# Value products by seven multiplications with a transfer each way, and other places for a difference, loads, pieces and last additions

## The chip, the cores and the metric

The kernel runs on one core of one Trainium2 chip. The metric is device time in microseconds (us) of that core. Its engines have their own instruction streams and meet through semaphores: PE (TensorE, matmuls; PEld its weight loads), DVE (VectorE), ACT (ScalarE), POOL (GpSimd) and SP (SyncE, which here only issues transfers). An engine's stream is in order: an instruction that waits holds all behind it.

## The reference, cut to what matters

```python
def reference(x, Wqkv, Wout, w1, w2, w3):          # x: 1 x 2048 x 256
    xn = layernorm(x)
    qkv = einsum('bsd,ed->bse', xn, Wqkv)          # 16 heads of 128: q, k, v
    logits = einsum('bqhd,bkhd->bhqk', q, k) * 128 ** -0.5
    out = einsum('bhqk,bkhd->bqhd', softmax(logits), v)
    attn = einsum('bse,de->bsd', out, Wout)
    ffn = bitlinear(sigmoid(bitlinear(xn, w1)) * bitlinear(xn, w2), w3)
    return x + attn + ffn
```

All in float32. The change concerns `v`, the values: for each head a 2048x256 by 256x128 product.

## The kernel before, in words

**Stages.** A lead-in loads x, normalizes and transposes it into `xnT` (256 channels as 2 x 128 partitions, 2048 tokens), computes the feed-forward part and the first heads' q, k and v. The main loop (L905 to L1025) goes over 63 of the 64 blocks, and the last one follows it (`last_weighted`). Block n is head n // 4 and a quarter of 512 queries; it has four steps t = 0 to 3 of 128 queries each. Two heads are a group of eight blocks; below, "block i" is i = n % 8 within its group, and block 8 is block 0 of the next group.

**One step** of the loop does for a step six ahead (`LEAD`) the scores (PE: 16 matmul instructions of 512 columns into two of three PSUM tiles; DVE: two maxima and nm; ACT: two exponentials), then `exchanged` (twelve transfers of 64 KB, ten on SP's queue and two on ACT's, and four copies on ACT, which carry 32-row pieces between partitions), two steps later `transposed` (DVE, two transposes of 128x1024 into `R`), and for the step itself `weighted` (PE, probabilities by values).

**Seven products for eight.** The weighted sum is done by a scheme of Strassen's kind (Winograd's form): a 2x2 split needs seven products in place of eight and sums of the operands. On the side of the probabilities these are the differences T1 to T4 (`differences`), on POOL, in place in `R` (seven slots of 128x2048; `roles` says which slot is a, b, c, d, e of a block). On the side of the values they are `v_combined` 0 to 3, into `st` and in place. PE needs T1 and T2 in step 1 of a block, T3 in step 2, T4 in step 3. A block's POOL program is: in step 3 of the block before T1 (first half), T3 (first half) and, where a head begins, `v_combined` 0 and 1; in step 0 `put_away` (a transfer that waits for DVE's last operation on the block before), T1 (second half), `spread` (a transfer that broadcasts the inverse sums), T3 (second half), T2 (low); in step 1 T2 (high), `v_combined` 2 and 3 where a head begins, T4; in step 2 the transfer of `inverses`, which waits for DVE.

**What lies beside.** Each step can take one or two more products on PE, through one PSUM bank (`ps_m`, one buffer, so that a product waits until DVE has read the one before it). Steps 2 and 3 make the next head's q and k, by seven products as well (`fast_product`, `fast_read`, with sums of weights `ws` and of x `t0`, `t2`, made once by `x_sums`). Steps 0 and 1 make output products of the group before in blocks 0 to 3 (`o_product`), and the next group's values in blocks 4 to 7: `v_product` (L261), one a step, gives 256 tokens by 256 columns, for both heads, straight with tokens on partitions; `v_read` (L271) copies it into the two heads' value tiles.

A product's first half is issued inside `beside`, behind the step's scores; its second (`twice`) at the step's end, and the read of the second in `left` (`behind`), at the start of the next step, ahead of which comes `added` (DVE: the sum of the copied halves into `oU`, and in step 3 the multiplication by the inverses).

**Other things touched.** `between` (L875) issues most of POOL's transfers behind step t: weights, `o_fetched`, `y_moved`, and towards the end `fetched_back` (part sums back into `xnT`) and `x_fetched`. `first` (L869) places pieces of the first heads' q, k and v in the lead-in's last steps.

Of the kernel before, what the change touches and what calls it, by code (L numbers as in the profile page):

```python
# [9 lines left out]
F32 = mybir.dt.float32  # L10
F32R = mybir.dt.float32r
AF = mybir.ActivationFunctionType
ALU = mybir.AluOpType
# [7 lines left out]
def layernorm_attention_bitffn_kernel(  # L21
# [14 lines left out]
    nc = tc.nc  # L36
    P = 128
    S, DM = x.shape
    FF = w1T.shape[1]
    D = P  # L40
# [10 lines left out]
    G = 2  # L51
# [93 lines left out]
    def weight_sums(h: int):  # L145
# [6 lines left out]
        nc.gpsimd.tensor_tensor(w[:, 3], wk[:, 1], w[:, 1], sub)  # L152
        ws[h] = w

    def x_sums(c: int):
        t = apool.tile([P, 4, QB], F32, tag=f"t{c}", name=f"t{c}", bufs=1)
        x00, x10 = (xnT[:, d, bass.ts(c, QB)] for d in range(KC))
        x01, x11 = (xnT[:, d, bass.ts(c + 1, QB)] for d in range(KC))
        for i, (a, b) in enumerate(((x01, x00), (x11, t[:, 0]), (x11, x01), (x10, t[:, 1]))):
            nc.gpsimd.tensor_tensor(t[:, i], a, b, ALU.subtract)  # L160
        ts[c] = t

    def fast_product(h: int, b: int, i: int, second: bool):

        c = b // 2 * 2
        wk, wq = (weights[h // G, i][:, :, bass.ts(h % G, D)] for i in "kq")
        w, t = ws[h], ts[c]
        x00, x10 = (xnT[:, d, bass.ts(c, QB)] for d in range(KC))
        x11 = xnT[:, 1, bass.ts(c + 1, QB)]
        lhs, rhs = {  # L170
            (0, 0): ((wk[:, 0], x00), (w[:, 1], t[:, 1])),
            (0, 1): ((w[:, 2], t[:, 2]), (wq[:, 1], t[:, 3])),
            (1, 0): ((w[:, 0], t[:, 0]), (w[:, 3], x11)),
            (1, 1): ((wk[:, 1], x10),),
        }[b % 2, i][second]
        pm = ps_m.tile([P, QB], F32, tag="m", name=f"pw{h}_{b}_{i}_{int(second)}")
        in_halves(pm, lhs, rhs, True, True)
        return pm

    def fast_read(h: int, b: int, i: int, second: bool, pm):  # L180
        c = b // 2 * 2
        if (b % 2, i) == (0, 0):
            if not second:
                if c == 0:
                    kTs[h] = kvpool.tile([P, S], F32, tag="kT", name=f"kT{h}")
                for j in range(2):
                    qTs[h, c + j] = kvpool.tile(
                        [P, QB], F32, tag="qT", name=f"qT{h}_{c + j}", bufs=NB + 2
                    )
        k0, k1 = (  # L190
            kTs[h].rearrange("p (j k r) -> p k j r", j=P // 32, r=32)[:, j * TB : (j + 1) * TB]
            for j in (c, c + 1)
        )
        q0, q1 = qTs[h, c], qTs[h, c + 1]
        pk = pm.rearrange("p (k j r) -> p k j r", j=P // 32, r=32)
        def q_sum(q, base):
            nc.vector.tensor_tensor(q, pm, base, ALU.add)  # L197

        def k_sum(k, base):
            nc.vector.tensor_tensor(k, pk, base, ALU.add)  # L200

        if (b % 2, i) == (0, 0):
            if not second:
                nc.vector.tensor_copy(k0, pk)
            else:
                k_sum(k1, k0)
        elif (b % 2, i) == (0, 1):
            if not second:
                nc.vector.tensor_tensor(
                    q1.rearrange("p (k j r) -> p k j r", j=P // 32, r=32), pk, k1, ALU.add  # L210
                )
            else:
                q_sum(q0, q1)
        elif (b % 2, i) == (1, 0):
            if not second:
                q_sum(q1, q1)
            k_sum(k1, k1)
        else:
            k_sum(k0, k0)
# [38 lines left out]

    def v_product(g: int, m: int, second: bool):  # L261
        w = weights[g, "v"]
        pm = ps_m.tile([P, 2, G * D], F32, tag="m", name=f"pvw{g}_{m}")
        for j in range(2):
            for d in range(KC):
                in_halves(
                    pm[:, j], xnT[:, d, bass.ts(2 * m + j, P)], w[:, d], d == 0, d == KC - 1
                )
        return pm

    def v_read(g: int, m: int, second: bool, pm):  # L271
        for j in range(G):
            nc.vector.tensor_copy(
                v_tile(g * G + j)[:, 2 * m : 2 * m + 2], pm[:, :, bass.ts(j, D)]
            )

    ppool = ctx.enter_context(tc.tile_pool(name="ppool", bufs=2))
    front = ExitStack()
# [7 lines left out]
    ods = [  # L286
        [away.tile([P, G, QB], F32, tag=f"od{g}_{c}", name=f"od{g}_{c}") for c in range(NB)]
        for g in range(2)
    ]
    rds = [away.tile([P, 32], F32, tag=f"rd{i}", name=f"rd{i}") for i in range(2)]  # L290

# [292 lines left out]
    def exchanged(v: int):  # L584
        ps = exps.pop(v)
        parts[v] = [
            ppool.tile([P, 2, S // NQ], F32, tag=f"part{i}", name=f"part{v}_{i}") for i in range(2)
        ]


        todo = [(j + 2 * a, g + 2 * i) for a in range(2) for i in range(2) for j in range(2) for g in range(2)]
        def ends(j, g):
            return (
                parts[v][g // 2][bass.ts(j, 32), g % 2, :],
                ps[j // 2][bass.ts(g, 32), bass.ts(j % 2, S // NQ)],
            )

        for m, (j, g) in enumerate((j, g) for j, g in todo if j != g):
            queue = nc.sync if m < SP_DMAS else nc.scalar
            if v > len(blocks) * TB - 3:  # L600

                queue = (nc.sync, nc.scalar)[m % 2]
            queue.dma_start(*ends(j, g))  # L603
        for j in range(NQ):
            nc.scalar.copy(*ends(j, j))  # L605
# [227 lines left out]
    def projected(n: int, u: int, pool=ps_m, tag: str = "m"):  # L833
# [34 lines left out]

    first = {  # L869
        1: [("v", 0, NV - 1), ("k", 1, 0)], 2: [("k", 1, 1), ("q", 0, NB - 1)],  # L870
        3: [("k", 1, 2), ("q", 1, 1)], 4: [("k", 1, 3), ("q", 1, 2)], 5: [("v", 0, NV - 2)],
    }
    made = {("q", 1, 0)} | {p for todo in first.values() for p in todo}

    def between(n: int, t: int):  # L875

        g, i = divmod(n, GB)
        last = NBK - NB

        if t == 1:  # L880
            if i == NB - 1 and g + 1 < H // G:
                load_weights(g + 1, "v", nc.gpsimd)
            elif i == GB - 1 and n < last or n == last - 1:
                load_weights(g, "o", nc.gpsimd)
        if g and i < NB:
            if t == 0 and i + 1 < NB:
                y_moved(i + 1, False)
            elif t == 1 and i + 1 < NB:
                o_fetched(g - 1, i + 1)
        elif n < last:  # L890
            if (i, t) == ((GB - 2, 2) if g else (GB - 1, 2)):
                y_moved(0, False)
            if (i, t) == (GB - 2, 3):
                o_fetched(g, 0)
        if n >= last - 1 and t == (1 if n < last else 2):
            b = n + 1 - last
            nc.gpsimd.dma_start(o3[:, b % 2], ods[(H - 2) // G % 2][b][:, 0])
        if (n, t) in ((last - 2, 3), (last - 1, 2)):
            fetched_back(n + 2 - last)
        if t == 0 and n in (last - 3, last - 2, last, last + 1):  # L900
            x_fetched((last - 3, last - 2, last, last + 1).index(n))

    behind = []
    with tc.manual_schedule():
        for u in range(-LEAD, (NBK - 1) * TB):  # L905
# [13 lines left out]
            if n >= NB and t < 2:  # L919
                i, j = divmod(i, NB)  # L920
                j = 2 * j + t
                if not i:
                    seven, hi = True, (g - 1, j)
                    product, read, twice = o_product, o_read, False
                elif g + 1 < H // G:
                    seven, hi = True, (g + 1, j)
                    product, read, twice = v_product, v_read, False
            pms = []

            def beside():  # L930
# [10 lines left out]
            if t == 0 and n >= 0:  # L941
                if 0 < n <= NBK - NB:
                    put_away(n - 1)
                differences(n, "T1b")
                spread(n)
                differences(n, "T3b")
            elif t == 1 and n >= 0:
                differences(n, "T2h")
                if blocks[n][1] == 0:
                    v_combined(blocks[n][0], 2)  # L950
                    v_combined(blocks[n][0], 3)
                differences(n, "T4")
            elif t == 3 and -1 <= n < NBK - 2:
# [1 line left out]
                if n % GB < NB <= n < NBK - NB - 2:  # L955
                    y_moved(n % GB, True)
                differences(n + 1, "T3a")
                if n >= 0 and blocks[n + 1][1] == 0:
                    v_combined(blocks[n + 1][0], 0)
                    v_combined(blocks[n + 1][0], 1)  # L960
            if more:
# [21 lines left out]
                elif v % TB == 1 and ("q", 1, b) not in made:  # L983
                    q_piece(1, b)
            if b == NB - 1 and h + 2 < H:
                if h % G == 0 and v % TB in (0, 2):
                    load_weights(h // G + 1, "qk"[v % TB // 2], nc.gpsimd)
                if v % TB == 3:
                    weight_sums(h + 2)
            twice = seven and twice  # L990
# [21 lines left out]
            if more:  # L1012
                exchanged(v)
            if v == NBK * TB + 1:
                transposed(v - 3)
                transposed(v - 2)
            if t == 2 and n > NBK - NB:
# [7 lines left out]
                between(n, t)  # L1025

        n = NBK - 1
        behind.pop()()
        for k in range(NKT):
            last_weighted(k, 0)  # L1030
            if k in (KQ - 1, 3 * KQ - 1):
# [47 lines left out]
```

## Time and profile before

| what | value |
|---|---|
| runs | 2183.15, 2184.22, 2187.87 us; median 2184.22 |
| the profiled execution | 2184.97 us; its span, first to last instruction, 2183.2 us |
| granted clock of PE, mean | 0.998 |
| DVE transposes `R<-part`, 128x1024, x512 | 605.2 us busy, 1220 ns each |
| DVE `kT<-pw,kT`, 128x512 from PSUM, x112 | 76.9 us busy, 686 ns each |
| DVE `v<-pvw`, 128x256 from PSUM, x112 | 42.0 us busy, 417 ns each |
| POOL differences `R<-R`, 128x1024 and 128x2048, x441 | 1176.6 us busy |
| POOL waiting for DVE's `oU` before `od<-oU` | 192.6 us in 60 blocks |
| transfers on POOL's queue, 512 KB: `o<-od`, `osums<-yd`, `yd<-osums` | 4.2, 4.3, 3.4 us to landing (medians) |
| transfers `part<-p`, 64 KB, x2552 on SP and x520 on ACT | 2.2 and 2.1 us to landing |

A line of a timeline or a group reads: start and duration in us, engine, line of the code, operation, out<-in by the program's names, shapes, how many; in brackets the idle time before it and what ended it. A line of the list of waits reads: engine, what waited, what it waited for; us in all, times, the longest. Matmuls are pipelined and their ends are modelled, so PE's starts say more than its busy time. float32 matmuls appear as two instructions, and a product that is issued in two halves of 64 columns as four.

### The profile page before, as it was taken

The numbers are of one execution on the slowest core, as the hardware profiler recorded it, in microseconds if no ns is written. First come the engines' busy times: TensorE is split into PE (matmuls) and PEld (weight loads), VectorE is DVE, ScalarE is ACT, GpSimd is POOL, SyncE is SP. The second block draws the span as 40 slices with busy tenths as digits, with TensorE's granted clock in tenths as the row PEclk, the third lists the DMA queues.
The fourth block names the chain that finished last, engine by engine and source line by source line (L and its number), as shares of the span: only waits on it lengthen the run. The fifth ranks groups of instructions, "written<-read, shape, count | busy, mean of one in ns | idle before, by whom it ended". The sixth has DMA issues, their size and how long they took to land. (4 is left out here: it accounts for less than half of the span.)

```text
span 2183.2 us, 41234 instructions
## 1 busy us (share of the span) xinstructions
PE 2160.2 (99%) x14074; PEld 1412.8 (65%) x14074; DVE 1725.5 (79%) x2338; ACT 1374.6 (63%) x2414; POOL 1472.0 (67%) x884
## 2 busy tenths in 40 slices
PE   9998999999999999999999999999999999999998
PEld 6744567776666666666666666666666665666665
DVE  6567887888887887888788788788788878888774
ACT  5586666666666666666666666666666666666662
POOL 0067767767667766767777776786766777677772
PEclk9999999999999999999999999999999999999999
DMA  2155545665556655566555654566555665556652
GB/s 93 41 115 138 124 112 136 159 170 134 120 138 164 163 129 124 142 170 156 122 135 143 175 144 113 135 159 172 130 118 138 173 160 126 126 141 175 168 144 80
DMA packets 180771, 300.65 MB, mean 138 GB/s; under 512 B 54416, under 2 KB 59920, under 8 KB 180560
## 3 DMA queue, kind: packets, MB, share of 16 engines
q1 hardware_dynamic: 127472, 174.69, 31.7%
q0 software_dynamic: 27152, 88.30, 15.9%
q10 hardware_dynamic: 25936, 35.03, 6.4%
q8 instruction: 111, 1.82, 0.4%
q14 instruction: 100, 0.82, 0.1%
HBM read 61.93 MB, written 34.54 MB: 44 GB/s over the span
## 5 line engine op out<-in xcount | busy, mean ns | idle before, releaser
L669 POOL TENSOR_TENSOR R<-R 128x1024 f32<-128x1024 f32 x441 | 1176.6, 2679 | 115.5 <-DVE R L649 100.4
L94 PE MATMUL s<-kT,qT 128*64 128x512 f32 x4000 | 953.2, 593 | 2.1 <-ACT p L578 2.1
L605 ACT COPY part<-p 32x512 f32<-32x512 f32 x1024 | 630.7, 616 | 394.8 <-issue 269.9
L568 DVE TENSOR_REDUCE mx<-s 128x1 f32<-128x1024 f32 x512 | 620.6, 1222 | 300.7 <-PE s L94 287.1
L94 PEld LDWEIGHTS s<-kT,qT 128*64 128x64 f32 x4000 | 502.9, 137 | 308.5 <-issue 80.9
L578 ACT ACTIVATE p<-s,nm 128x1024 f32<-128x1024 f32 x512 | 565.9, 1110 | 209.1 <-PE pw L94 105.7
L649 DVE STREAM_TRANSPOSE R<-part 128x1024 f32<-128x1024 f32 x512 | 605.2, 1220 | 15.1 <-DMA part<-p 13.1
L716 PE MATMUL av<-R,v 128*64 128x256 f32 x3728 | 551.0, 379 | 0.1
L716 PE MATMUL av<-R,st 128*64 128x256 f32 x3024 | 471.7, 379 | 11.0 <-POOL R L669 9.0
L716 PEld LDWEIGHTS av<-R,v 128*64 128x64 f32 x3728 | 363.4, 137 | 160.3 <-issue 8.8
L716 PEld LDWEIGHTS av<-R,st 128*64 128x64 f32 x3024 | 304.2, 137 | 97.3 <-POOL R L669 13.0
L620 POOL DMA_DIRECT2D rd<-r x60 | 33.7, 562 | 233.9 <-DVE r L619 233.9
L734 ACT COPY oU<-av 64x256 f32<-64x256 f32 x248 | 90.7, 366 | 127.0 <-PE av L716 124.6
L772 POOL DMA_DIRECT2D od<-oU x60 | 34.0, 567 | 195.1 <-DVE oU L746 192.6
L742 DVE TENSOR_TENSOR oU<-av,oU 64x256 f32<-64x256 f32 x248 | 102.2, 412 | 45.5 <-ACT oU L734 42.8
L94 PE MATMUL pvw<-wv,xnT 128*64 128x256 f32 x896 | 117.7, 379 | 0.0
L94 PE MATMUL pow<-o,wo 128*64 128x512 f32 x448 | 116.1, 592 | 0.0
L94 PEld LDWEIGHTS pvw<-wv,xnT 128*64 128x64 f32 x896 | 78.6, 137 | 42.3 <-DVE qT L197 5.2
L94 PE MATMUL pw<-t,ws 128*64 128x512 f32 x336 | 105.3, 592 | 0.0
L578 ACT ACTIVATION_READ_ACCUMULATOR p<-s,nm 128x1 f32 x512 | 100.3, 196 | 0.0
L94 PEld LDWEIGHTS pow<-o,wo 128*64 128x64 f32 x448 | 58.9, 137 | 37.3 <-issue 5.4
L200 DVE TENSOR_TENSOR kT<-pw,kT 128x512 f32<-128x512 f32 x112 | 76.9, 686 | 1.7
(146 smaller groups left out, 1332.2 us busy)
## 6 DMA issues: line engine op xcount, KB each, us to landing
part<-p SPq DMA_DIRECT2D x2552, 64.0 KB, 2.2
part<-p ACTq DMA_DIRECT2D x520, 64.0 KB, 2.1
oT<-rd POOLq DMA_DIRECT2D x60, 256.0 KB, 5.6
od<-oU POOLq DMA_DIRECT2D x60, 256.0 KB, 2.7
o<-od POOLq DMA_DIRECT2D x28, 512.0 KB, 4.2
osums<-yd POOLq DMA_DIRECT2D x28, 512.0 KB, 4.3
yd<-osums POOLq DMA_DIRECT2D x26, 512.0 KB, 3.4
yd<-yT SPq DMA_DIRECT2D x4, 512.0 KB, 2.6
```

What stands on the lines that cost most here:

```text
L94: nc.tensor.matmul(out[c * HP : (c + 1) * HP], lhs[:, c * HP : (c + 1) * HP], rhs, start=start, stop=stop, skip_group_check=True,)
L200: nc.vector.tensor_tensor(k, pk, base, ALU.add)
L568: nc.vector.tensor_reduce(mx[:, i : i + 1], s, AX.X, ALU.max)
L578: nc.scalar.activation(p, s, AF.Exp, bias=nm, scale=SCALE, accum_out=sums[n][:, t, i : i + 1],)
L605: nc.scalar.copy(*ends(j, j))
L620: nc.gpsimd.dma_start(rds[n % 2], riT)
L649: nc.vector.transpose(to[:, t % 2, 2 * i : 2 * i + 2], part.rearrange("p g (s c) -> p g s c", s=2),)
L669: nc.gpsimd.tensor_tensor(o, x, y, ALU.subtract)
L716: nc.tensor.matmul(av[i * HP : (i + 1) * HP, half], l[:, kk], moving(s, kk), start=start, stop=(k == units[r] - 1), skip_group_check=True,)
L734: nc.scalar.copy(u[op, oq], av[ap, half])
L742: nc.vector.tensor_tensor(u[p, q], av[p, half], u[p, q], ALU.add)
L772: nc.gpsimd.dma_start(ods[h // G % 2][b][:, h % G], oU)
```

## The change

The values of a group are made by seven products for each half of the tokens (1024), in the form of `fast_product`: `fast_v_product`, with weight sums made by `v_sums` on POOL (four operations on 128x128) in step 3 of block 3, and the x sums that exist. A product is 128 channels by 512 tokens, so values come out with channels on partitions. `fast_v_read` adds each into the value tiles (eight operations of 128x512 a half). Then each head's half is turned: `v_sent` writes it to DRAM (512 KB, rows interleaved), `v_landed` reads it back into a part of `xnT` that is no longer read (`landing`: channels 0 to 127 of tokens 512 to 1535), both on POOL's queue, and `v_transposed` transposes its 32x32 blocks on DVE (two operations of 128x512). One landing place serves all four halves of a group, in turn; `v_steps` places them from block 5, step 1, to block 8, step 3. To leave tokens 512 to 1535 free, the second pair of token quarters is used in reverse order (`pair`).

Besides: `v_combined` 0 and 1 of a group's first head come after its last `v_transposed`; T3 (second half) and `spread` go from step 0 to step 1, behind T2 (high); the load of `wk` goes one step earlier; in the lead-in a piece of v and one of k change places; `fetched_back` and two loads into `o3` near the end go to other steps; the last `left` comes before the last transposes; the last two steps' exchanges use the queues as all others do.

```diff
+    def pair(c: int):
+        return (c, c + 1) if c == 0 else (c + 1, c)
...
-    def v_product(g: int, m: int, second: bool):
-        w = weights[g, "v"]
-        pm = ps_m.tile([P, 2, G * D], F32, tag="m", name=f"pvw{g}_{m}")
-        for j in range(2):
-            for d in range(KC):
-                in_halves(
-                    pm[:, j], xnT[:, d, bass.ts(2 * m + j, P)], w[:, d], d == 0, d == KC - 1
-                )
+    def sums_of(k, q, name: str):
+        w = wpool.tile([P, 4, D], F32, tag="wx", name=name)
+        nc.gpsimd.tensor_tensor(w[:, 0], q[:, 0], q[:, 1], ALU.add)
+        nc.gpsimd.tensor_tensor(w[:, 1], w[:, 0], k[:, 0], ALU.subtract)
+        nc.gpsimd.tensor_tensor(w[:, 2], k[:, 0], q[:, 0], ALU.subtract)
+        nc.gpsimd.tensor_tensor(w[:, 3], k[:, 1], w[:, 1], ALU.subtract)
+        wxs[name] = w
+    def fast_v_product(g: int, m: int, second: bool):
+        half, m = divmod(m, NB)
+        wv, w, t = weights[g, "v"], wxs[f"wvs{g}"], ts[2 * half]
+        c0, c1 = pair(2 * half)
+        x00, x10 = (xnT[:, d, bass.ts(c0, QB)] for d in range(KC))
+        x11 = xnT[:, 1, bass.ts(c1, QB)]
+        lhs, rhs = (
+            ((wv[:, 0, D:], x00), (w[:, 1], t[:, 1])),
+            ((w[:, 2], t[:, 2]), (wv[:, 1, :D], t[:, 3])),
+            ((w[:, 0], t[:, 0]), (w[:, 3], x11)),
+            ((wv[:, 1, D:], x10),),
+        )[m][second]
+        pm = ps_m.tile([P, QB], F32, tag="m", name=f"pvw{g}_{half}_{m}_{int(second)}")
+        in_halves(pm, lhs, rhs, True, True)
         return pm
...
+        todo = {
+            (0, True): ((k1, k0),), (1, False): ((q1, k1),), (1, True): ((q0, q1),),
+            (2, False): ((q1, q1), (k1, k1)), (2, True): ((k1, k1),), (3, False): ((k0, k0),),
+        }[m, second]
+        for o, i in todo:
+            nc.vector.tensor_tensor(o, pm, i, ALU.add)
+    def v_sent(h: int, half: int):
+        v = v_half(h, half).rearrange("p k d -> p (k d)")
+        nc.gpsimd.dma_start(
+            vds[h % G][half].rearrange("(r q) x -> q r x", q=P // 32), v
+        )
+    def v_landed(h: int, half: int):
+        nc.gpsimd.dma_start(landing, vds[h % G][half].rearrange("p (j c) -> j p c", j=P // 32))
+    def v_transposed(h: int, half: int):
+        v = v_half(h, half).rearrange("p k (q r) -> p q k r", r=32)
+        w = landing.rearrange("p (q k r) -> p q k r", q=P // 32, r=32)
+        for u in range(2):
+            nc.vector.transpose(v[:, 2 * u : 2 * u + 2], w[:, 2 * u : 2 * u + 2])
+    wxs, landing = {}, xnT[:, 0, QB : 3 * QB]
...
-            if v > len(blocks) * TB - 3:
-                queue = (nc.sync, nc.scalar)[m % 2]
...
-        3: [("k", 1, 2), ("q", 1, 1)], 4: [("k", 1, 3), ("q", 1, 2)], 5: [("v", 0, NV - 2)],
+        3: [("k", 1, 2), ("q", 1, 1)], 4: [("v", 0, NV - 2), ("q", 1, 2)], 5: [("k", 1, 3)],
...
+        v_steps = {
+            (5, 1): [(v_sent, 0, 0)], (5, 2): [(v_landed, 0, 0)],
+            (5, 3): [(v_transposed, 0, 0), (v_sent, 1, 0)],
+            (6, 1): [(v_landed, 1, 0)], (6, 2): [(v_transposed, 1, 0)],
+            (7, 1): [(v_sent, 0, 1)], (7, 2): [(v_landed, 0, 1)], (7, 3): [(v_transposed, 0, 1)],
+            (8, 1): [(v_sent, 1, 1)], (8, 2): [(v_landed, 1, 1)], (8, 3): [(v_transposed, 1, 1)],
+        }
...
+        for late in range(2):
+            if late < g + 1 < H // G + late:
+                for do, j, half in v_steps.get((i + late * GB, t), ()):
+                    do((g + 1 - late) * G + j, half)
+        if t == 3 and i == GB - 1 and g + 1 < H // G:
+            v_combined((g + 1) * G, 0)
+            v_combined((g + 1) * G, 1)
-        if n >= last - 1 and t == (1 if n < last else 2):
+        if n >= last - 1 and t == 2:
...
+        if t == 3:
+            if i == NB - 1 and g + 1 < H // G:
+                v_sums(g + 1)
-        if (n, t) in ((last - 2, 3), (last - 1, 2)):
+        if (n, t) in ((last - 2, 3), (last - 1, 0)):
             fetched_back(n + 2 - last)
...
-                    product, read, twice = v_product, v_read, False
+                    product, read, twice = fast_v_product, fast_v_read, j % NB != NB - 1
...
                 differences(n, "T1b")
-                spread(n)
-                differences(n, "T3b")
             elif t == 1 and n >= 0:
                 differences(n, "T2h")
+                differences(n, "T3b")
+                spread(n)
...
-                if n >= 0 and blocks[n + 1][1] == 0:
+                if n >= 0 and (n + 1) % GB == NB:
                     v_combined(blocks[n + 1][0], 0)
                     v_combined(blocks[n + 1][0], 1)
...
-                if h % G == 0 and v % TB in (0, 2):
-                    load_weights(h // G + 1, "qk"[v % TB // 2], nc.gpsimd)
+                if h % G == 0 and v % TB in (0, 1):
+                    load_weights(h // G + 1, "qk"[v % TB], nc.gpsimd)
...
             if v == NBK * TB + 1:
+                behind.pop()()
                 transposed(v - 3)
                 transposed(v - 2)
...
-        behind.pop()()
```

More of the change, by code (lines that the diff above doesn't have):

```diff
@@ L153, in weight_sums @@
         ws[h] = w
+    def pair(c: int):
+        return (c, c + 1) if c == 0 else (c + 1, c)
     def x_sums(c: int):
         t = apool.tile([P, 4, QB], F32, tag=f"t{c}", name=f"t{c}", bufs=1)
-        x00, x10 = (xnT[:, d, bass.ts(c, QB)] for d in range(KC))
-        x01, x11 = (xnT[:, d, bass.ts(c + 1, QB)] for d in range(KC))
+        c0, c1 = pair(c)
+        x00, x10 = (xnT[:, d, bass.ts(c0, QB)] for d in range(KC))
+        x01, x11 = (xnT[:, d, bass.ts(c1, QB)] for d in range(KC))
         for i, (a, b) in enumerate(((x01, x00), (x11, t[:, 0]), (x11, x01), (x10, t[:, 1]))):
@@ L167, in fast_product @@
         w, t = ws[h], ts[c]
-        x00, x10 = (xnT[:, d, bass.ts(c, QB)] for d in range(KC))
-        x11 = xnT[:, 1, bass.ts(c + 1, QB)]
+        c0, c1 = pair(c)
+        x00, x10 = (xnT[:, d, bass.ts(c0, QB)] for d in range(KC))
+        x11 = xnT[:, 1, bass.ts(c1, QB)]
         lhs, rhs = {
@@ L191, in fast_read @@
             kTs[h].rearrange("p (j k r) -> p k j r", j=P // 32, r=32)[:, j * TB : (j + 1) * TB]
-            for j in (c, c + 1)
+            for j in pair(c)
         )
-        q0, q1 = qTs[h, c], qTs[h, c + 1]
+        q0, q1 = (qTs[h, j] for j in pair(c))
         pk = pm.rearrange("p (k j r) -> p k j r", j=P // 32, r=32)
@@ L255, in v_place, with v_sums @@
         return (k + NKT // 2) % NKT if h == 1 else k
-    def v_product(g: int, m: int, second: bool):
-        w = weights[g, "v"]
-        pm = ps_m.tile([P, 2, G * D], F32, tag="m", name=f"pvw{g}_{m}")
-        for j in range(2):
-            for d in range(KC):
-                in_halves(
-                    pm[:, j], xnT[:, d, bass.ts(2 * m + j, P)], w[:, d], d == 0, d == KC - 1
-                )
-        return pm
[L271 to L274, printed above, removed]
-            )
+    def v_sums(g: int):
+        wv = weights[g, "v"]
+        sums_of(wv[:, :, D:], wv[:, :, :D], f"wvs{g}")
@@ new lines, in sums_of @@
+    def sums_of(k, q, name: str):
[9 more added lines that the diff above has]
+        c0, c1 = pair(2 * half)
+        x00, x10 = (xnT[:, d, bass.ts(c0, QB)] for d in range(KC))
+        x11 = xnT[:, 1, bass.ts(c1, QB)]
+        lhs, rhs = (
[6 more added lines that the diff above has]
+        in_halves(pm, lhs, rhs, True, True)
+        return pm
@@ new lines, in v_half, with fast_v_read @@
+    def v_half(h: int, half: int):
+        return v_tile(h)[:, half * NKT // 2 : (half + 1) * NKT // 2]
+    def fast_v_read(g: int, m: int, second: bool, pm):
+        half, m = divmod(m, NB)
+        q, k = (
+            v_half(g * G + i, half).rearrange("p k d -> p (k d)").rearrange(
+                "p (j k r) -> p k j r", j=P // 32, r=32
+            )
+            for i in range(G)
+        )
+        k0, k1, q0, q1 = (
+            i[:, j % 2 * TB : (j % 2 + 1) * TB] for i in (k, q) for j in pair(2 * half)
+        )
+        pm = pm.rearrange("p (k j r) -> p k j r", j=P // 32, r=32)
+        if (m, second) == (0, False):
+            nc.vector.tensor_copy(k0, pm)
+            return
+        todo = {
[4 more added lines that the diff above has]
+            nc.vector.tensor_tensor(o, pm, i, ALU.add)
@@ new lines, in v_sent @@
+    def v_sent(h: int, half: int):
+        v = v_half(h, half).rearrange("p k d -> p (k d)")
+        nc.gpsimd.dma_start(
+            vds[h % G][half].rearrange("(r q) x -> q r x", q=P // 32), v
+        )
+    def v_landed(h: int, half: int):
[5 more added lines that the diff above has]
+            nc.vector.transpose(v[:, 2 * u : 2 * u + 2], w[:, 2 * u : 2 * u + 2])
@@ L288, in layernorm_attention_bitffn_kernel @@
         for g in range(2)
+    ]
+    vds = [
+        [away.tile([P, S // 2], F32, tag=f"vd{h}{i}", name=f"vd{h}{i}") for i in range(2)]
+        for h in range(G)
     ]
```

## The prediction

> **What bounds the kernel now.** I read the page's busy line first, then the list of waits, then the timelines of the places where the change acts.
>
> ```profile
> PE 2160.2 (99%) x14074; PEld 1412.8 (65%) x14074; DVE 1725.5 (79%) x2338; ACT 1374.6 (63%) x2414; POOL 1472.0 (67%) x884
> ...
> L94 PE MATMUL pvw<-wv,xnT 128*64 128x256 f32 x896 | 117.7, 379 | 0.0
> ```
>
> PE is the bound: time falls only if PE gets less work or loses a stall. The list of waits says how few stalls there are, and which reads are just in time:
>
> ```profile
> PE av L716 <- POOL R L669: 9.0, 8, 3.3
> ...
> PEld pow L94 <- DVE qT L197: 4.6, 13, 0.4
> ```
>
> PE's starts give each product's price better than its busy time, since matmuls overlap:
>
> ```profile
> 305.89 2.09 PE L94 MATMUL pvw<-wv,xnT 128*64 128x256 f32 x16
> 307.62 3.82 PE L716 MATMUL av<-R,st 128*64 128x256 f32 x32
> ...
> 641.60 1.23 PE L94 MATMUL pw<-xnT,ws 128*64 128x512 f32 x4
> 642.46 3.80 PE L94 MATMUL s<-kT,qT 128*64 128x512 f32 x16
> ```
>
> A value product of before takes 307.62 - 305.89 = 1.73 us; one 128x512 product of the kind that replaces it takes 642.46 - 641.60 = 0.86.
>
> **PE's products.** Before: 7 groups x 8 x 1.73 = 96.9 us. After: 7 x 14 x 0.86 = 84.3. **-12.6 us**.
>
> **Second difference ahead of the third.** In blocks 0 to 3 no value or output product lies beside steps 0 and 1, and PE reaches step 1 before POOL has T2:
>
> ```profile
> 203.44 2.39 POOL L669 TENSOR_TENSOR R<-R 128x1024 f32<-128x1024 f32 x1
> 205.78 0.78 POOL L626 DMA_DIRECT2D oT<-rd  x1
> 206.57 2.37 POOL L669 TENSOR_TENSOR R<-R 128x1024 f32<-128x1024 f32 x1
> ...
> 212.03 1.95 PE L716 MATMUL av<-R,st 128*64 128x256 f32 x16 [3.29 <-POOL R L669]
> ```
>
> These are T1b, the spread and T3b; T2 comes after them. From the first weighted matmul of step 1 to the next scores PE takes 6.3, 6.1, 7.6 and 4.6 us in blocks 0 to 3 (148.24 to 154.55, 177.19 to 183.29, 208.14 to 215.69, 241.71 to 246.29) where 3.45 is normal: 10.7 us lost. With T2 at once after T1b it is 0.78 + 2.37 = 3.15 us earlier. What stays is about 1.7 us in block 2, whose start is held by the load of wq, still waiting for PE's pq, and now by wk (0.73) ahead of put_away. T3b and the spread, now in step 1, are needed at step 2 and at the end of step 3; T4 ends as late as before. **-9 us** (-10.7 to -4). The exchange of the value piece with the key piece lets v_combined start without its 1.85 us wait; PE isn't behind it then.
>
> **The end.**
>
> ```profile
> 2067.40 3.61 PE L94 MATMUL s<-kT,qT 128*64 128x512 f32 x8 [2.15 <-ACT p L578]
> ...
> 2158.42 1.08 PE L94 MATMUL po<-wo,oU 128*64 128x256 f32 x8 [1.99 <-DVE oU L742]
> ```
>
> At 2158.42 PE waits for the last additions, queued on DVE behind four transposes (2153.29 to 2157.91). The additions go ahead of them; the transposes then end some 2 us later, 7 before the second half of the last block reads them (2167). After that wait the granted clock is 0.53 for 3.5 us, another 1.65: **-4** (0 to -4). At 2067.40 ACT was 3 us late with its copies, held by transfers: wo, o and xnT (1 MB in all) were issued at 2053.9 to 2055.2. Now they are spread over three steps (xnT<-yd, 0.7 us of POOL, goes ahead of T2's second half there, which gained 3.15). The wait and the slow clock after it (0.55 for 3.8 us) cost 3.9; I take **-3** (0 to -3.9). Four exchange transfers of each of the last two steps move from ACT's queue to SP's: 4 x 0.6 = 2.4 us later, under the same 7 us.
>
> **DVE's reads.** 112 copies of 417 ns become 112 operations on 128x512; the row of kT<-pw,kT says 686, so +30 us over 56 steps. Most steps 0 and 1 have room (DVE idles 0.9 to 2.2 us before reductions). Product T (the second of a step) needs the one PSUM bank after the first's read, at 302.46 in block 5; the read with two additions ends there at 299.5 + 1.4: nothing.
>
> **DVE's transposes, new.** Eight 128x512 a group. The rows are 1220 ns for 128x1024 and 211 for 128x32, on a line 0.65 to 0.7; a pair is 1.3 us. Four places a group:
> (i) end of step 3 in blocks 5 and 7: the next products there have 0.7 us or more left: nothing.
> (ii) end of step 2 in block 6: the read ahead of the second product of step 3 ended 357.43, PE needs it at 357.54; 0.7 us of DVE's idle takes half of the delay; about 0.5 us of stall x 7 = **+3.5** (0 to +9).
> (iii) end of step 3 in block 8, here block 16:
>
> ```profile
> 680.11 2.36 DVE L649 STREAM_TRANSPOSE R<-part 128x1024 f32<-128x1024 f32 x2
> ...
> 683.69 0.69 DVE L197 TENSOR_TENSOR qT<-pw,qT 128x512 f32<-128x512 f32 x1
> ```
>
> DVE is gapless from 678.12 to 686.6, and PE's output product starts at 684.59, 0.2 us after that read ended; it is the wait of 13 times above. 1.3 us more ahead of the read passes through: 1.15 x 7 = **+8** (0 to +9).
>
> **The transfers, and who is behind them.** The tightest are those of block 8:
>
> ```profile
> 648.16 1.29 POOL L691 TENSOR_TENSOR st<-v 128x512 f32<-128x512 f32 x1
> ...
> 652.13 0.57 POOL L772 DMA_DIRECT2D od<-oU  x1 [1.32 <-DVE oU L746]
> ...
> 670.31 0.57 POOL L780 DMA_DIRECT2D o<-od  x1
> 672.42 0.55 POOL L620 DMA_DIRECT2D rd<-r  x1 [1.54 <-DVE r L619]
> ```
>
> The first two v_combined now wait for the transposes that follow DVE's step 3, done at 650.65 + 1.3 = 651.95, not 648.16. They end 654.6, put_away moves from 652.1 to 654.6, and the chain on POOL without a pause (T1b, T2, osums<-yd, T3b, spread, v_combined, T4) ends at 672.9, not 670.4. T2 still ends at 662.8; PE wants its second half at 663.96. After o<-od, v_sent goes out at 673.5. v_landed must wait for its landing, and POOL stands: behind it are T1a, yd<-osums and T3a, covered by the 4.06 us that POOL waits for DVE at 683.96. Landing rows for 512 KB: yd<-osums 3.4 us, osums<-yd 4.2. 673.5 + 3.4 + 4.2 plus 0.3 of issue = 681.4, before DVE's 682.47; the worst rows (6.9 and 7.5, among other loads) give 688.2, 5.7 late. Behind o<-od it will not be the best: I take 0.4 us of wait x 7 = **+3** (0 to +40). In blocks 5 to 7 v_landed has 2 us or more to spare.
>
> [...]
>
> **At nothing:** v_sums (4 x 0.456 on POOL in step 3 of block 3) has 0.85 us of POOL's wait at 523.02 and the 3.15 that T2 gained; uncovered, 1 us x 7. pair() only renames operands. wk's load goes a step earlier, off T2's path, behind the last reader of wk in the same step.
>
> **Sum:** -12.6 - 9 - 4 - 3 + 3.5 + 8 + 3 = -14.1. The profiled execution took 2184.97 (span 2183.2 and 1.8 around it), 0.75 above the median: 2170.9 there, **2170** beside the median.
>
> **Rivals.**
> *The value chain becomes the bound (slower).* Place: step 0 of the block after each group's first, where PE's output product waits for DVE's read behind the transposes behind the landing. 2.6 us of landing wait + 1.15 + 1.7 of slow clock = 5.5 x 7 = 38.5; with -28.6 of gains and +3.5 that is +13.4: **2198**. It decides from (28.6 - 3.5) / 7 = 3.6 us a group. For it: 1 MB is issued within 0.6 us there, as at 2054, and another follows. Against: osums<-yd mostly landed in 4.0 to 4.4 us.
> On the clock, the trace shows 0.55 after a wait of 2.15 us (2067.2 to 2071) but 1.00 after one of 3.29 (210 to 215). [...]
> *All is absorbed.* Losses (ii), (iii) and landings find slack: -28.6, **2156**. Against: the 13 waits on qT.
> *The spread in step 1 slows the exchanges.* Beside oT<-rd part transfers land in 6 us (332.01, 428.37), not 2.2; now these are transposed in the short step 3. 0.2 us in 60 blocks = +12: **2182**. Against: two steps lie between.
> *It doesn't do what it says:* if the landing in xnT's spare columns held every product that reads xnT, 28 x 4 us = +112. Against: R is one tile too, and its parts are waited for apart.
>
> **Chances.** Forecast 0.47 (2160 to 2180), chain 0.24, absorbed 0.14, exchanges 0.13, not as said 0.02. Below 0.2% (4.4 us) a measurement can't tell a change from none. Faster 0.65: forecast and absorbed, less what lies above 2179.8, and a third of the exchanges. Same 0.10. Slower 0.25: the chain less its mildest part, and the last case. The range 2153 to 2192 leaves out the worse half of the chain.
>
> **What would show it.** Right: pvw products 0.86 us apart; no PE wait on POOL R in blocks 0 to 3; none at the last po; PE's output product in the second block of groups 1 to 7 waiting 1 to 2 us for DVE's qT; DVE's new transposes waiting for landing in block 8 alone. Wrong: that wait beyond 3.6 us, a granted clock of half in each group, T2 late in block 8, or SP backed up in step 3.

## The result, and the profile after

The changed kernel takes **2536.99 us** (median of 6 runs, 2524.59 to 2541.78), against 2186.35 (2183.15 to 2188.07, 6 runs) of the kernel before: ratio 1.1596, 95% interval 1.1569 to 1.1623. It is 16% slower where 0.6% faster was forecast (2170 us, range 2153 to 2192). Profiled was an execution of 2524.59 us, span 2522.8. Nearly all of the difference has one source, the time that two new transfers take to land.

The page of the changed kernel, busy time of the engines and the clock that PE was granted in 40 slices:

```profile
PE 2209.9 (88%) x13570; PEld 1048.9 (42%) x13570; DVE 1796.0 (71%) x2394; ACT 1378.7 (55%) x2414; POOL 1553.5 (62%) x968
...
PEclk9999989899898998989989899989999799998999
```

PE has 504 matmul instructions fewer, as planned, and is busy 88% of the span in place of 99%: it waits for some 313 us. The list of waits of the changed kernel says for whom (what waited, for what; us in all, times, the longest):

```profile
DVE v L335 <- DMA xnT<-vd: 308.7, 28, 19.8
...
PE av L780 <- DVE oU L806: 129.0, 17, 11.6
...
POOL xnT L329 <- DMA vd<-v: 121.0, 14, 13.4
PE pow L94 <- DVE qT L202: 118.6, 7, 20.6
...
PE pw L94 <- DVE kT L205: 50.0, 8, 9.9
```

Begin with what the others depend on. DVE's new transposes wait for the landing 28 times of 28, for 308.7 us. PE's three waits are for additions and reads that stand on DVE behind these transposes; together 297.6 us. The wait of PE on POOL's differences, 9.0 us in 8 times before, is gone. What lands so late is in the table of transfers (operation, how many, KB each, median us from issue to landing):

```profile
part<-p SPq DMA_DIRECT2D x2560, 64.0 KB, 2.5
...
vd<-v POOLq DMA_DIRECT2D x28, 512.0 KB, 11.4
xnT<-vd POOLq DMA_DIRECT2D x28, 512.0 KB, 12.9
...
yd<-osums POOLq DMA_DIRECT2D x26, 512.0 KB, 3.5
```

Three transfers of 512 KB on one queue in one execution: 11.4, 12.9 and 3.5 us. Size and queue don't explain the first two. One half's way through the engines, POOL, DVE and PE of the changed kernel in block 5 of the first group:

```profile
306.00 0.75 POOL L324 DMA_DIRECT2D vd<-v  x1
...
317.17 1.60 POOL L329 DMA_DIRECT2D xnT<-vd  x1 [5.74 <-DMA vd<-v]
```

```profile
319.32 2.37 DVE L713 STREAM_TRANSPOSE R<-part 128x1024 f32<-128x1024 f32 x2 [1.28 <-DMA part<-p]
329.89 1.30 DVE L335 STREAM_TRANSPOSE v<-xnT 128x512 f32<-128x512 f32 x2 [8.20 <-DMA xnT<-vd]
331.23 0.43 DVE L806 TENSOR_TENSOR oU<-av,oU 64x256 f32<-64x256 f32 x1
```

```profile
322.46 1.03 PE L94 MATMUL pvw<-xnT,wv 128*64 128x512 f32 x4
331.71 4.53 PE L780 MATMUL av<-R,osums 128*64 128x256 f32 x20 [8.22 <-DVE oU L806]
```

The send is issued at 306.00 and has landed when POOL gets on at 317.17; the fetch is issued there and lands at 329.9. From then on nothing else is late: transposes, addition, and PE starts 0.05 us after the addition's record ends, 8.22 us late. This happens four times a group, in blocks 5 to 8, each time a half lands. Each wait costs PE its clock too: in the 3.3 us after each of the 28 waits (5.3 to 20.6 us long) the granted clock is 0.50 to 0.58. Stretches of the changed kernel (from and to, length, busy us of each engine with its instructions, granted clock, DMA share, GB/s):

```profile
20.00:300.00 280.00, 275.47 (x1452) 154.46 (x1453) 207.72 (x281) 191.47 (x333) 142.15 (x84) 1.00 0.39 95
...
390.00:520.00 130.00, 102.07 (x626) 45.71 (x624) 82.19 (x107) 62.55 (x111) 78.52 (x50) 0.89 0.56 142
```

Ahead of the first `vd<-v` the clock is 1.00 and PE is busy 98%; later in the loop 0.89 and 79%.

### The profile page after: what moved, and what is told of

Same layout as the page of the kernel before. It is cut to its first block, busy times and chain, and to the rows that moved or that the text cites. A ratio compares the mean times of both kernels' runs of the same rounds, so it can differ in the third digit from the quotient of the medians.

```text
span 2522.8 us, 40452 instructions
## 1 busy us (share of the span) xinstructions
PE 2209.9 (88%) x13570; PEld 1048.9 (42%) x13570; DVE 1796.0 (71%) x2394; ACT 1378.7 (55%) x2414; POOL 1553.5 (62%) x968
## 5 line engine op out<-in xcount | busy, mean ns | idle before, releaser
L94 PE MATMUL s<-kT,qT 128*64 128x512 f32 x4000 | 902.3, 592 | 6.4 <-ACT p L645 6.4
L780 PE MATMUL av<-R,v 128*64 128x256 f32 x3728 | 567.1, 404 | 119.6 <-DVE oU L806 119.5
L94 PEld LDWEIGHTS s<-kT,qT 128*64 128x64 f32 x4000 | 285.7, 137 | 528.8 <-issue 470.0
L780 PEld LDWEIGHTS av<-R,v 128*64 128x64 f32 x3728 | 343.5, 147 | 301.7 <-DVE oU L806 132.7
L780 PE MATMUL av<-R,st 128*64 128x256 f32 x3024 | 456.2, 379 | 2.1 <-DVE oU L806 1.3
L780 PEld LDWEIGHTS av<-R,st 128*64 128x64 f32 x3024 | 282.1, 137 | 202.0 <-issue 69.1
L335 DVE STREAM_TRANSPOSE v<-xnT 128x512 f32<-128x512 f32 x56 | 36.5, 690 | 308.7 <-DMA xnT<-vd 308.7
L94 PE MATMUL pow<-o,wo 128*64 128x512 f32 x448 | 117.8, 651 | 118.6 <-DVE qT L202 118.6
L329 POOL DMA_DIRECT2D xnT<-vd x28 | 44.8, 1599 | 170.1 <-DMA vd<-v 121.0
L94 PE MATMUL pw<-t,ws 128*64 128x512 f32 x336 | 92.9, 633 | 50.0 <-DVE kT L205 50.0
L94 PEld LDWEIGHTS pow<-o,wo 128*64 128x64 f32 x448 | 33.3, 147 | 189.6 <-DVE qT L202 126.9
## 6 DMA issues: line engine op xcount, KB each, us to landing
vd<-v POOLq DMA_DIRECT2D x28, 512.0 KB, 11.4
xnT<-vd POOLq DMA_DIRECT2D x28, 512.0 KB, 12.9
```

What stands on the lines that cost most here:

```text
L94: nc.tensor.matmul(out[c * HP : (c + 1) * HP], lhs[:, c * HP : (c + 1) * HP], rhs, start=start, stop=stop, skip_group_check=True,)
L329: nc.gpsimd.dma_start(landing, vds[h % G][half].rearrange("p (j c) -> j p c", j=P // 32))
L335: nc.vector.transpose(v[:, 2 * u : 2 * u + 2], w[:, 2 * u : 2 * u + 2])
L780: nc.tensor.matmul(av[i * HP : (i + 1) * HP, half], l[:, kk], moving(s, kk), start=start, stop=(k == units[r] - 1), skip_group_check=True,)
```

## The experiments

**Are the transfers slow by their shape?** Both go through an access pattern whose outermost dimension is 4: `v_sent` writes to `"(r q) x -> q r x"` with 4 for q, `v_landed` reads `"p (j c) -> j p c"` with 4 for j. The trace can't name the engine of a packet, but its records tell how many packets of 4096 bytes on POOL's queue are under way at one time. Where no other such transfer lies beside, that is 3.1 during `vd<-v` and 3.2 during `xnT<-vd` here (medians), over 9.2 and 9.4 us, against 12.3 during `osums<-yd` and 13.1 during `yd<-osums` in the trace of before, over 2.3 and 1.6 us. One packet takes 0.23 us here and 0.17 to 0.22 there: the packets are hardly slower, but fewer are under way. "Few engines" in the expectations below is the author's guess at the reason; no trace here shows it. What the runs test is the shape.

`split_both`: each as four transfers of 32 partitions.

```diff
-        nc.gpsimd.dma_start(vds[h % G][half].rearrange("(r q) x -> q r x", q=P // 32), v)
+        to = vds[h % G][half].rearrange("(r q) x -> q r x", q=P // 32)
+        for q in range(P // 32):
+            nc.gpsimd.dma_start(to[q], v[bass.ts(q, 32)])
...
-        nc.gpsimd.dma_start(landing, vds[h % G][half].rearrange("p (j c) -> j p c", j=P // 32))
+        src = vds[h % G][half].rearrange("(r q) (j c) -> j r q c", q=P // 32, j=P // 32)
+        for j in range(P // 32):
+            nc.gpsimd.dma_start(landing[bass.ts(j, 32)].rearrange("r (q c) -> r q c", q=P // 32), src[j])
```

> The changed kernel with each of the two transfers issued as four, by 32 partitions (sent) and by 32 partitions (landed): the same bytes to the same places in the same pieces, but the outermost dimension of each access pattern is 32, not 4. [...] Rival (layout: the 1 KB pieces and interleaved rows in DRAM are what is slow): a whole one still takes over 10 us, and the kernel 2500 us or more, as eight issues now cost POOL 2 to 4 us more each.

`four_and_one`: the send in four, which now does the whole rearrangement in DRAM; the landing one plain transfer with 128 outermost.

```diff
-        nc.gpsimd.dma_start(vds[h % G][half].rearrange("(r q) x -> q r x", q=P // 32), v)
+        to = vds[h % G][half].rearrange("(j r) (q c) -> q r j c", j=P // 32, q=P // 32)
+        for q in range(P // 32):
+            nc.gpsimd.dma_start(to[q], v[bass.ts(q, 32)].rearrange("r (j c) -> r j c", j=P // 32))
...
-        nc.gpsimd.dma_start(landing, vds[h % G][half].rearrange("p (j c) -> j p c", j=P // 32))
+        nc.gpsimd.dma_start(landing, vds[h % G][half])
```

> The changed kernel with the whole rearrangement in the sending transfers (four, of 32 partitions, 1 KB pieces into DRAM) and the landing as one plain transfer of 128 rows of 4 KB. Theory (few engines): the landing transfer takes some 4.2 us as osums<-yd does, the four sent ones 3 to 5; 2160 to 2185 us. Rival (layout): the landing alone gets short, the four sent ones stay over 10 us; about 2350 us, since half of the wait is gone.

Measured: `split_both` 2209.94 us, ratio 1.0109 [1.0094, 1.0124], 20 us above the 2160 to 2190 that the author expected; `four_and_one` 2185.45, ratio 1.0003 [0.9988, 1.0019], at the upper end. (Ratios are to the kernel before, measured beside each run; in brackets the 95% interval.) The transfers of `four_and_one`:

```profile
vd<-v POOLq DMA_DIRECT2D x112, 128.0 KB, 3.5
xnT<-vd POOLq DMA_DIRECT2D x28, 512.0 KB, 4.3
```

The same bytes go the same way in 3.5 and 4.3 us, and 350 us are gone with it. `split_both` is 24.5 us slower than `four_and_one` with 3.4 and 3.6 us a transfer. It issues eight a half in place of five on POOL, which is busy 1608 us there against 1565, and DVE's idle time ahead of its new transposes is 33.6 us there against 16.9; that the issues are the reason isn't tested.

Two more runs take size and direction apart. `plain_sent` sends straight (128 outermost) and leaves the fetch as changed; `split_in_two` halves each transfer but has 2 outermost.

```diff
-            vds[h % G][half].rearrange("(r q) x -> q r x", q=P // 32), v
+            vds[h % G][half], v
```

> The changed kernel with v_sent writing partition p to row p: one transfer of 512 KB as in the change, the same 4 KB rows and the same DRAM tile, but the outermost dimension of the target is 128. The values land in another order, so the output is not the reference's. Theory (few engines): v_sent lands 3.4 to 4.5 us after its issue, v_landed still 12 to 13; the kernel takes about 2350 us. Rival (large transfers on POOL's queue into this tile are slow as such): both stay at 11 to 13 us, and the kernel at 2530.

```diff
+        to = vds[h % G][half].rearrange("(r q) x -> q r x", q=P // 32)
+        for i in range(2):
+            nc.gpsimd.dma_start(to[2 * i : 2 * i + 2], v[bass.ts(i, P // 2)])
...
+        src = vds[h % G][half].rearrange("p (j c) -> j p c", j=P // 32)
+        for i in range(2):
+            nc.gpsimd.dma_start(landing[bass.ts(i, P // 2)], src[2 * i : 2 * i + 2])
```

> The changed kernel with each transfer issued as two of 256 KB, each over two of the four values of the outermost dimension. [...] Rival (smaller transfers simply land faster, which would also explain split_both): 6 to 7 us to landing, about 2350 us.

Measured, one run each: `plain_sent` 2392.27 us, some 40 above what was expected, `split_in_two` 2599.05, where over 2480 was expected. Their transfers, first of `plain_sent`, then of `split_in_two`:

```profile
vd<-v POOLq DMA_DIRECT2D x28, 512.0 KB, 5.0
xnT<-vd POOLq DMA_DIRECT2D x28, 512.0 KB, 13.1
```

```profile
vd<-v POOLq DMA_DIRECT2D x56, 256.0 KB, 11.3
xnT<-vd POOLq DMA_DIRECT2D x56, 256.0 KB, 12.9
```

The straight send falls from 11.4 to 5.0 us with its 512 KB, and half the bytes through a pattern with 2 outermost take as long as all through one with 4. The packets go with it: 12.6 are under way during `vd<-v` of `plain_sent`, over 1.8 us, and 3.1 in `split_in_two`, over 9.2 us, for its two pieces together. So in these kernels it is the outermost dimension, not the bytes of a transfer. Which engines carry the packets the trace doesn't show, so why the time goes with this dimension stays open; the packets under way and these four kernels are the evidence.

**What the rest of the change is worth.** `no_transfer` leaves both transfers out and keeps the transposes, products and everything else; `others_only` is the kernel before with all but the new values; `t2_first` the kernel before with T2 and the order of step 0 and 1 alone.

```diff
 def v_sent
-        nc.gpsimd.dma_start(...)
+        pass
 def v_landed
-        nc.gpsimd.dma_start(...)
+        pass
```

> The changed kernel without v_sent and v_landed: v_transposed transposes what lies in the landing place, so the values of groups 1 to 7 are not the reference's. Everything else is as in the change. Theory (the transfers' landing is all that went wrong): 2155 to 2172 us, by the prediction's sum without its +3 for landings 2167; PE still waits 1 to 1.3 us a group for DVE's qT in the second block (the prediction's place iii), and has no wait over 2 us in the middle of the kernel. Rival (DVE's transposes, the products or the moved differences cost as well): over 2200 us.

```diff
-                spread(n)
-                differences(n, "T3b")
             elif t == 1 and n >= 0:
                 differences(n, "T2h")
+                differences(n, "T3b")
+                spread(n)
...
-        if n >= last - 1 and t == (1 if n < last else 2):
+        if n >= last - 1 and t == 2:
...
-        if (n, t) in ((last - 2, 3), (last - 1, 2)):
+        if (n, t) in ((last - 2, 3), (last - 1, 0)):
...
             if v == NBK * TB + 1:
+                behind.pop()()
...
-        behind.pop()()
```

> The kernel before with all edits of the change but the values: T2 ahead of T3b and the spread, the load of wk a step earlier, pieces, loads near the end, last additions, queues of the last two steps. The prediction's terms for these are -9 (blocks 0 to 3), -4 (last additions) and -3 (loads near the end): 2168 us, and no PE wait on POOL R in blocks 0 to 3. Rival (the spread in step 1 slows the exchanges): 2180 us or more.

`t2_first` is the first piece of that diff on its own.

> The kernel before with one edit: T2 (high) ahead of T3b and the spread. The prediction's term for blocks 0 to 3 is -9 us (-10.7 to -4), so 2174 to 2177 us, with no PE wait on POOL R in blocks 0 to 3 and the waits near the end as before. If the rest of others_only's 18.7 us were not the end's, this would be under 2170.

Measured: `no_transfer` 2160.45 us, ratio 0.9888 [0.9874, 0.9903]; `others_only` 2166.29, 0.9915 [0.9901, 0.993]; `t2_first` 2172.37, 0.9946 [0.9932, 0.9961]. In `t2_first` PE no longer waits for POOL's differences in blocks 0 to 3. POOL there, in block 2:

```profile
201.20 2.37 POOL L669 TENSOR_TENSOR R<-R 128x1024 f32<-128x1024 f32 x1
203.51 0.73 POOL L83 DMA_DIRECT2D wk<-in_wqkvT_dram  x1
204.27 7.02 POOL L669 TENSOR_TENSOR R<-R 128x1024 f32<-128x1024 f32 x3
211.24 0.78 POOL L626 DMA_DIRECT2D oT<-rd  x1
```

T2's second half is now one of the differences from 204.27 on, next to its first, and the spread comes behind it. In `no_transfer` one wait of PE in each group is left, the one at step 0 of the group's second block:

```profile
416.44 1.94 PE L94 MATMUL pow<-o,wo 128*64 128x512 f32 x8 [0.67 <-DVE qT L202]
```

By PE's starts it is 1.05 to 1.07 us long in all seven groups: the last transposes, 1.3 us on DVE ahead of the read, with nothing to wait for themselves.

**Why do normal transfers still cost 25 us?** `four_and_one` lands in 4.3 us and is 25.0 us above `no_transfer`. Its list of waits has `PE pow L94 <- DVE qT L202: 20.6, 7, 4.1`, the same place. DVE and PE of `four_and_one` there:

```profile
415.63 1.30 DVE L337 STREAM_TRANSPOSE v<-xnT 128x512 f32<-128x512 f32 x2 [1.58 <-DMA xnT<-vd]
...
417.43 0.69 DVE L812 TENSOR_TENSOR oU<-oU,oT 128x512 f32<-128x512 f32 x1
```

```profile
418.90 2.69 PE L94 MATMUL pow<-o,wo 128*64 128x512 f32 x8 [2.37 <-DVE qT L202]
```

In all seven groups the last transposes wait here for the landing, 1.0 to 3.4 us, together 14.9. This one wait of PE is 15.9 us longer than in `no_transfer` (4.7 in the list), and PE's busy time over the whole kernel 8.3 us longer (2151.5 against 2143.2), together 24.2 of the 25 us. In the 3.3 us after the wait the granted clock is 0.50 to 0.66 in four of the groups and 1.00 in three.

`late_last` is `four_and_one` with the last transposes two steps later, in step 1 of the group's second block:

```diff
-            (8, 1): [(v_sent, 1, 1)], (8, 2): [(v_landed, 1, 1)], (8, 3): [(v_transposed, 1, 1)],
+            (8, 1): [(v_sent, 1, 1)], (8, 2): [(v_landed, 1, 1)], (9, 1): [(v_transposed, 1, 1)],
```

> four_and_one with the last of a group's transposes (second head, second half) in step 1 of block 9 instead of step 3 of block 8, so that it no longer stands before DVE's read that PE's output product waits for. These values are needed in block 12 only. Theory (what is left of the loss is that one place): PE's waits for DVE's qT, 20.6 us in four_and_one, fall under 2; with the 4.7 us of them that no_transfer still had also gone, 2152 to 2160 us, faster than the kernel before by 1.1 to 1.5% and than others_only (2166). Rival (the transfers cost by their traffic on the DMA engines, wherever they are waited for): no better than 2170 us.

Measured: 2172.64 us, ratio 0.9943 [0.9925, 0.9962], short of what was expected. The transposes are gone from the place, and PE still waits 2.2 to 2.6 us there in each group. PE, DVE and POOL of `late_last` at that place:

```profile
422.82 3.23 PE L94 MATMUL pow<-o,wo 128*64 128x512 f32 x8 [2.25 <-DVE qT L202]
```

```profile
418.31 0.43 DVE L808 TENSOR_TENSOR oU<-av,oU 64x256 f32<-64x256 f32 x1
418.77 3.26 DVE L812 TENSOR_TENSOR oU<-oU,oT 128x512 f32<-128x512 f32 x1
422.07 0.69 DVE L202 TENSOR_TENSOR qT<-pw,qT 128x512 f32<-128x512 f32 x1
```

```profile
415.66 0.55 POOL L331 DMA_DIRECT2D xnT<-vd  x1 [3.38 <-DVE nm L640]
416.23 2.39 POOL L735 TENSOR_TENSOR R<-R 128x1024 f32<-128x1024 f32 x1
418.56 0.55 POOL L850 DMA_DIRECT2D yd<-osums  x1
419.12 2.36 POOL L735 TENSOR_TENSOR R<-R 128x1024 f32<-128x1024 f32 x1
```

A DVE operation that takes 0.69 us in most of its 60 places, and at this place in `four_and_one`, takes 3.26, and ends 0.56 after POOL's subtraction of 419.12. So the move itself brought the second wait about: without the transposes ahead of it the add comes earlier against POOL's work, beside the subtraction. (POOL's 3.38 of idle is put down to DVE, which had long been done: it is `v_landed` waiting for the send's landing.) By the records the add starts 0.1 to 0.4 us ahead of the subtraction in all seven groups and is held all the same. It starts inside POOL's issue of `yd<-osums` each time (418.56 here), and whether that issue has a part in it isn't tested. `landed_later` is `late_last` with the landing's issue moved behind POOL's T1 and T3:

```diff
-            (8, 1): [(v_sent, 1, 1)], (8, 2): [(v_landed, 1, 1)], (9, 1): [(v_transposed, 1, 1)],
+            (8, 1): [(v_sent, 1, 1)], (8, 3): [(v_landed, 1, 1)], (9, 1): [(v_transposed, 1, 1)],
```

> late_last with one thing moved: the last landing is issued on POOL at the end of step 3 of the group's first block, behind the next block's T1a, yd<-osums and T3a, and not at the end of step 2 ahead of them. In late_last POOL stood 3.38 us (412.27 to 415.66) for vd<-v ahead of xnT<-vd, T3a went to 419.12 to 421.48, and DVE's oU<-oU,oT, which reads two SBUF operands as T3a does, took 3.26 us from 418.77 to 422.04, 0.56 after T3a's end, where it takes 0.69 elsewhere; in all seven groups that add takes 3.0 to 3.3. Theory: DVE's add is held while POOL's subtraction runs, and that is the whole stall of 2.2 to 2.6 us on PE's output product; with T3a some 3.5 us earlier the add takes 0.69, the wait on qT falls from 14.1 us to under 3, and the time from 2172.6 to 2154 to 2160. Rival: the stall comes with the transfers' own traffic (ACT's copies and the exchanges late), whoever stands ahead on POOL: the add may be short, but PE still loses 2 us a group there and the time stays above 2168.

Measured: **2159.82 us** (4 runs), ratio 0.9882 [0.9865, 0.9898], the fastest of all. DVE, POOL and PE of `landed_later` at the place:

```profile
417.57 0.69 DVE L812 TENSOR_TENSOR oU<-oU,oT 128x512 f32<-128x512 f32 x1
418.30 0.69 DVE L202 TENSOR_TENSOR qT<-pw,qT 128x512 f32<-128x512 f32 x1
```

```profile
413.93 2.39 POOL L735 TENSOR_TENSOR R<-R 128x1024 f32<-128x1024 f32 x1
416.25 0.57 POOL L331 DMA_DIRECT2D xnT<-vd  x1
```

```profile
415.69 3.60 PE L94 MATMUL s<-kT,qT 128*64 128x512 f32 x16
419.12 1.89 PE L94 MATMUL pow<-o,wo 128*64 128x512 f32 x8
```

POOL's subtraction ends before the add begins, the add takes 0.69, and PE doesn't wait. That the add is long beside POOL's work is shown, 3.26 us against 0.69; what holds it there is not. The add also meets POOL's work at step 3 of block 7, where beside `st<-v` it takes 1.41 us in each group (1.39 to 1.40 in the changed kernel); PE has room there and loses nothing.

## Why the prediction was wrong, point by point

- **The step that failed: "Landing rows for 512 KB: yd<-osums 3.4 us, osums<-yd 4.2."** These rows were taken for the new transfers because bytes and queue were the same. The new ones have 4 as their outermost dimension, which the diff showed in both `rearrange` calls, the rows 128 partitions, and they took 11.4 and 12.9 us. The wait at block 8 was put at +3 (0 to +40), and with it fell "In blocks 5 to 7 v_landed has 2 us or more to spare": 8.0 and 8.7 us more (by the 4.2; the row of `osums<-yd` itself says 4.3) made all four places of a group waits. Shown by `four_and_one`, where only the shape and the number of the transfers differ, and for the send alone by `plain_sent`. Compared with `landed_later`, which makes the same products in 2159.82 us, the changed kernel loses 377 us, 364 between the two profiled executions. Of these 297.6 are PE's three waits, and its busy time for the same 13,570 instructions is 2209.9 us against 2144.5, another 65, which goes with the lower clock. The division between the two is by the profile, not by a run.
- **The rival named the right mechanism.** "The value chain becomes the bound", landing, transposes, read, PE's wait, and then the slow clock, is what the trace shows; it was given 0.24. Its price, 38.5 us, came from the same rows, and it saw one place a group where there were four.
- **Even with the rows as forecast the term was too small.** `four_and_one` lands in 3.5 and 4.3 us and stands 25.0 us above `no_transfer`, inside 0 to +40 but not +3. The 0.4 us of wait for the landing at block 8 was 2.1 in the mean, and 15.9 of the 25 us are PE's longer wait there. Some of it may come from the three more issues that the send in four costs POOL (0.56 us each), which the prediction did not have; how much is not measured. A held add has no part in these 25 us: it takes 0.69 us there in six groups and 0.85 in one. With the transposes moved and the add clear of the subtraction, `landed_later` is within 0.7 us of `no_transfer`. The latter still has 7.4 us of waits behind the transposes (place (iii) below), so the transfers should cost some 7 us yet, give or take the few us of the intervals. Some 3 are in the lists of waits, PE waiting for DVE's kT, qT and oU in short pieces (4.0 us against 0.6); where the rest lies stays open.
- **PE's products, -12.6: right.** By PE's starts, 96.8 us of value products before, 84.2 in `landed_later`.
- **T2 ahead of T3b, -9, and the end, -4 and -3: right in sum, -16.0 forecast, -18.7 measured** (2184.99 to 2166.29). `t2_first` alone gave -13.1 (8.5 to 14.9 by its interval), where the bound was 10.7: the wait on ACT at 2067.40, counted under the loads at the end, went with it. So moving T2 was enough to win what had been put down to the loads. Its -3.9 off, -9.2 stays for blocks 0 to 3. What is left for the other edits near the end is some 6, of which the additions' -4 is a part; a difference of two runs, it is uncertain by several us.
- **DVE's transposes.** Place (iii) was forecast at 1.15 x 7 = 8.0 and was 1.05 x 7 = 7.4 in `no_transfer`. Place (ii), +3.5, cost nothing there: no stall of PE at block 6. Place (i): nothing, as said.
- **The clock.** The value chain rival counted 1.7 us of slow clock behind each wait of 2.6 + 1.15 = 3.75 us. In the traces the length of a short wait didn't decide. After waits of 1.99, 2.15 and 2.18 us the clock fell to 0.53, 0.55 and 0.50, after 2.91, 2.99 and 3.29 it stayed at 1.00. (The first two and the last are of the kernel before, the others of `four_and_one`.) Only after the changed kernel's waits of over 5 us did it fall each time, to 0.50 to 0.58 in 28 of 28.
- **The spread in step 1** didn't slow the exchanges by anything that shows in `others_only`. "It doesn't do what it says", all readers of xnT held by the landing, didn't occur either: the stalls stand behind DVE.

## What to carry to other kernels

Before a duration is taken from another transfer's row, compare the outermost dimension of both access patterns as well as bytes and queue: with 4 there 512 KB took 11.4 and 12.9 us here, with 128 there 5.0 and 4.3. Put the partitions there, and if the rearrangement forbids it, cut the transfer along the short dimension into several (3.5 us a quarter in `four_and_one`). An operation on one engine can hold one on another though neither waits for the other's result: where an add on DVE and a subtraction on POOL come to lie in the same microseconds, look whether the add's duration is its usual one (here 3.03 to 3.29 us in place of 0.69). A wait that stays when its suspected cause has been moved may have got a new cause by the move, and the durations of the instructions there can say more than their idle time.

## What the runs showed that was not expected

- DVE's `oU<-oU,oT` of 128x512 took 3.03 to 3.29 us beside a POOL subtraction of 128x1024 in all seven groups of `late_last`, and 0.69 at the same place in all seven of `landed_later`. It appears as busy time of DVE, not as a wait, so no list of waits shows it.
- The issue of `xnT<-vd` with 4 outermost held POOL 1.60 us in the changed kernel, with 128 outermost 0.55 to 0.57. The issue of `vd<-v`, also with 4 outermost, took 0.74, so 4 alone doesn't set it; what does isn't tested.
- After a wait of 2.25 us PE's next eight matmuls took 3.23 us in `late_last` (422.82); the same eight without the wait 1.89 in `landed_later` (419.12); the granted clock was 0.58 and 1.00. A short stall can be paid again in the clock, but need not be: in `late_last` the clock fell behind this wait in two of the seven groups, and stayed at 1.00 in five.
